# The last chunk's normalisation on ScalarE and VectorE in place of GpSimd, stored by halves on two queues

## The chip, the cores and the metric

The kernel runs on one core of one Trainium2 chip. The metric is the device time of one execution in microseconds (us), taken outside the profiler; several executions are made and their median is quoted. A separate, profiled execution gives the rows that are read below. The engines are called by the profile's names: PE is TensorE (PEld its weight loads), DVE is VectorE, ACT is ScalarE, POOL is GpSimd, SP is SyncE, which here only issues transfers and waits. A "q" behind a name (POOLq, SPq) marks instructions that the engine's sequencer handles: waits, barriers, drains, issues of transfers.

## The reference

A transformer layer of two parts, each followed by a residual sum and a normalisation over the 512 columns of a row without learned parameters. The input x has 4 batches of 1024 rows of 512 columns, all in fp32.

```
def _layernorm(x, axis=-1, eps=1e-05):
    m = jnp.mean(x, axis=axis, keepdims=True)
    v = jnp.var(x, axis=axis, keepdims=True)
    return (x - m) / jnp.sqrt(v + eps)
...
    x = _layernorm(x + _L0_attn_ref(x, L0_attn_wq, L0_attn_wk, L0_attn_wv, L0_attn_wo), axis=-1)
    x = _layernorm(x + _L0_ffn_ref(x, L0_ffn_A, L0_ffn_B, L0_ffn_Wr, L0_ffn_br), axis=-1)
```

`_L0_attn_ref` is softmax attention with 16 heads of 32 columns. `_L0_ffn_ref` picks for each row the one of 8 experts with the largest router logit; an expert is a product down to 64 columns (A) and back up to 512 (B), weighted with the router's probability. What matters here is only the very last step of the second line: the second normalisation of the last rows.

## The kernel before

The kernel walks over units of (batch, group of four heads). A planner at the end of the function lays out steps; to each step it assigns matrix products of the attention and pieces of the projections and of the expert stage of earlier batches, so that TensorE always has work. The instructions of one engine run in the order in which the code emits them (`keep_order` ties them down).

For the first three batches the expert stage (`class After`) sorts rows by expert; its results go out with indirect stores issued by GpSimd (L649). For the last batch (`class Last`) the rows stay where they are. Its 1024 rows are handled in four chunks of 256 rows (`n` = 0 to 3, `NQ` = 4), each of two tiles of 128 rows (`i` = 0, 1). `down(i, half)` multiplies the masked inner values with the second expert matrix for one half of the columns (256, four matmuls, L743), and VectorE adds gate times result to the rows `h` (L747). In the first three chunks the norm follows for whole tiles. In the last chunk (`self.n == NQ - 1`, the code from L755 on) nothing is left to hide anything under, so the statistics are taken by halves: `bn_stats` on each half as it comes (L757), `bn_aggr` over both (L760) once the second half is there, giving mean and variance.

From there the norm before the change runs over three engines. VectorE negates the mean (L761). `finish_stats` on GpSimd adds eps (L407), raises to the power -0.5 (L408) and multiplies with the negated mean (L409). `apply` on ScalarE computes scale times h plus bias over all 512 columns (L419). `store` sends the 128x512 tile out on SyncE's queue (L766). Tile 0 of the last chunk goes through this while TensorE still multiplies for tile 1; tile 1 goes through it alone.

GpSimd's last work ahead of these two tiles are four indirect stores of the third batch (L649). After the last instruction of the kernel's body every engine runs a closing sequence that the framework adds, recorded under L1113: SyncE waits for every counter that a transfer or an engine still owes, one wait after the other; each engine drains; all meet at a barrier that GpSimd opens, which is followed by a reset of the semaphores and a second barrier.

On-chip memory is handed out by pools in the order of first use: `const` (one buffer each) and then `work` (two buffers unless stated). Sizes are rounded up to 32 bytes per partition.

Of the kernel before, what the change touches and what calls it, by code (L numbers as in the profile page):

```python
# [9 lines left out]
F32 = mybir.dt.float32  # L10
# [3 lines left out]
AF = mybir.ActivationFunctionType  # L14
ALU = mybir.AluOpType
# [3 lines left out]
P = 128  # L19
# [4 lines left out]
EPS = 1e-5  # L24
# [17 lines left out]
def attention_then_experts(  # L42
# [18 lines left out]
    pe, act, dve, pool, sync = nc.tensor, nc.scalar, nc.vector, nc.gpsimd, nc.sync  # L61
    B, S, D = x.shape
# [4 lines left out]
    TQ = QC // P  # L67
# [4 lines left out]
    H2 = D // 2  # L72
# [8 lines left out]
    const = ctx.enter_context(tc.tile_pool(name="const", bufs=1))  # L81
    work = ctx.enter_context(tc.tile_pool(name="work", bufs=2))
# [7 lines left out]
    def bank():  # L90
        turn_of[0] += 1
        return banks[(turn_of[0] - 1) % len(banks)]
# [31 lines left out]
    pool.memset(ones, 1.0)  # L124
    power = const.tile([P, TQ], F32, tag="power", name="power")
    pool.memset(power, -0.5)

    rev = const.tile([P, TQ, E], F32, tag="rev", name="rev")
    for e in range(E):
# [5 lines left out]
        out=before_f,  # L135
# [33 lines left out]
    for t in spread_m:  # L169
# [5 lines left out]
        out=expand_f,  # L175
# [226 lines left out]
    def finish_stats(mv):  # L402

        n = mv.shape[1]
        rs = work.tile([P, 2, TQ], F32, tag="rs", name="rs", bufs=4)[:, :, :n]
        var = work.tile([P, TQ], F32, tag="var", name="var")[:, :n]
        pool.tensor_scalar_add(var, mv[:, :, 1], EPS)  # L407
        pool.tensor_tensor(rs[:, 0], var, power[:, :n], ALU.pow)  # L408
        pool.tensor_tensor(rs[:, 1], mv[:, :, 0], rs[:, 0], ALU.mult)  # L409
        return rs  # L410
# [7 lines left out]
    def apply(h, rs, i):  # L418
        act.activation(h, h, AF.Identity, bias=rs[:, 1, i : i + 1], scale=rs[:, 0, i : i + 1])  # L419
# [42 lines left out]
    def stored(i):  # L462

        for other in stores:
            tc.declare_no_dep(i, other, reason="other rows")
        stores.append(i)

    class After:
# [159 lines left out]
        def down(self, k):  # L628
            tiles = [bank() for _ in range(2)]
            for i, ps in enumerate(tiles):  # L630
                pe.matmul(ps, self.u[k][ts(i, R), :], self.wb[k][ts(i, R), :], start=True, stop=True)  # L631
            for i, ps in enumerate(tiles):
                t = self.x[k, i]
                dve.scalar_tensor_tensor(t[:, :D], ps, t[:, D : D + 1], t[:, :D], ALU.mult, ALU.add)
# [35 lines left out]
    class Last:  # L670
# [69 lines left out]
        def down(self, i, half):  # L740
            ps = bank()[:, :H2]
            for k in range(C):
                pe.matmul(  # L743
                    ps, self.u[:, k, ts(i, P)], places["wd"][:, k, ts(half, H2)], start=(k == 0), stop=(k == C - 1)
                )
            h = self.h[i][:, ts(half, H2)]
            dve.scalar_tensor_tensor(h, ps, self.gate[:, i : i + 1], h, ALU.mult, ALU.add)  # L747
            if self.n < NQ - 1:
                if half == 1:
                    if i == 0:  # L750
                        self.mv = work.tile([P, TQ, 2], F32, tag="y_mv", name="y_mv2")
                    self.add(self.mv, i)
                return

            if half == 0:  # L755
                self.st = work.tile([P, 2, 6], F32, tag="st2", name="st2")
            dve.bn_stats(self.st[:, half, :], h)  # L757
            if half == 1:
                mv = work.tile([P, 1, 2], F32, tag="y_mv3", name="y_mv3")
                dve.bn_aggr(mv[:, 0, :], self.st)  # L760
                dve.tensor_scalar_mul(mv[:, 0, 0:1], mv[:, 0, 0:1], -1.0)  # L761
                apply(self.h[i], finish_stats(mv), 0)
                self.store(i)

        def store(self, i):
            stored(sync.dma_start(out[B - 1, ts(TQ * self.n + i, P), :], self.h[i]).ins)  # L766
# [116 lines left out]
    for b, r in enumerate(rest):  # L883
        end = start_of(C * b + C)
        for i in range(4):
            part = sorted_x[b].rearrange("(i j p) w -> i p j w", p=P, i=4)[i]
# [4 lines left out]
        for t in range(NT):  # L891
            n, i = divmod(t, TQ)
# [224 lines left out]
```

## Time and profile before

| what | value |
| --- | --- |
| median of 3 runs | 1482.48 us (1482.31 to 1485.71) |
| the profiled execution: time | 1484.24 us |
| the profiled execution: span from first to last instruction | 1482.5 us |
| granted TensorE clock, mean | 0.998 |
| start of VectorE's last sum (L747), behind the last matmul | 1473.07 us |
| end of ScalarE's last norm (L419) | 1476.36 us |
| issue of the last store (L766) | 1476.38 us |
| transfers in the last 43 us: SyncE's queue | 1.05 MB, 5.6% of 16 engines |

Times with two decimals are positions in the span of the profiled execution, in us from its first instruction. A row of the timeline gives start and length, then engine, line, operation, what is written and read, and in brackets how long the engine had been idle before it and who ended that. A row of an instruction group gives the shortest, median and longest length in ns and the first and last start. The time before is that of whole executions; the span is shorter than the profiled execution's time by what lies around it (1484.24 - 1482.5 = 1.7 us).

### The profile page before, as it was taken

How to read it: one execution, taken by the hardware profiler on the slowest of the kernel's cores; microseconds unless marked ns; L12 is line 12 of the kernel's file. 1: busy time of each engine (PE TensorE's matmuls, PEld its weight loads, DVE VectorE, ACT ScalarE, POOL GpSimd, SP SyncE). 2: the span in 40 equal slices, each digit the busy share in tenths (PEclk: the TensorE clock that was granted, in tenths of full speed). 3: DMA queues.
4: the chain of work that ended last, by engine and by line, in shares of the span. 5: the costliest groups of instructions: out<-in, count | busy, mean ns of one | idle time of the engine just before them, and what ended most of it. 6: DMA issues, size and time to landing. Idle time of an engine off the chain costs nothing.

```text
span 1482.5 us, 36966 instructions
## 1 busy us (share of the span) xinstructions
PE 1448.4 (98%) x15091; PEld 947.9 (64%) x15091; DVE 984.3 (66%) x1822; ACT 743.1 (50%) x1519; POOL 1170.3 (79%) x918
## 2 busy tenths in 40 slices
PE   8999999999999999999999999999999999999997
PEld 6666666666666666666666666666666655666665
DVE  1556666665767567776776656777676767777764
ACT  1125555554444555555444455555544555456552
POOL 2019999998977989999987888999997899999302
PEclk9999999999999999999999999999999999999999
DMA  7422121114001622433200333342411230222010
GB/s 242 137 82 81 47 70 60 56 44 155 18 30 41 193 90 86 130 100 123 73 16 29 101 122 101 119 130 88 158 30 30 73 115 23 69 74 70 20 37 29
DMA packets 93050, 122.09 MB, mean 82 GB/s; under 512 B 7607, under 2 KB 68039, under 8 KB 92880
## 3 DMA queue, kind: packets, MB, share of 16 engines
q1 hardware_dynamic: 84672, 103.93, 22.3%
q0 software_dynamic: 6096, 13.69, 2.5%
q8 instruction: 119, 1.95, 0.6%
q10 hardware_dynamic: 2112, 2.10, 0.4%
q14 instruction: 51, 0.42, 0.1%
HBM read 92.34 MB, written 33.63 MB: 85 GB/s over the span
## 4 chain that ended last, share of the span: by engine, by line
PE 84%; POOL 7%; ACT 4%; issue 2%; DMA 1%; DVE 1%; ACTq 0%; POOLq 0%; SPq 0%
PE bank L373 14%; PE bank L330 13%; PE bank L290 12%; PE bank L276 8%; PE bank L257 8%; PE bank L267 8%; PE bank L454 7%; POOL dens L358 5%; PE bank L321 5%; ACT probs L340 3%; PE bank L392 2%; PE bank L729 2%; PE bank L622 1%; PE bank L615 1%; PE bank L631 1%
## 5 line engine op out<-in xcount | busy, mean ns | idle before, releaser
L358 POOL TENSOR_TENSOR dens<-dens,probs 128x1024 f32<-128x1024 f32 x360 | 849.0, 2358 | 79.3 <-ACT probs L340 57.1
L292 DVE TENSOR_REDUCE top<-bank 128x1 f32<-128x512 f32 x1024 | 635.9, 683 | 407.5 <-PE bank L290 407.2
L340 ACT ACTIVATE probs<-bank 128x512 f32<-128x512 f32 x1024 | 528.1, 603 | 284.6 <-PE bank L330 264.7
L290 PE MATMUL bank<-k,q 32*128 32x512 f32 x2048 | 276.9, 593 | 0.0
L330 PE MATMUL bank<-q,k 32*128 32x256 f32 x4096 | 266.2, 374 | 0.0
L373 PE MATMUL bank<-probs,v 128*32 128x256 f32 x4096 | 234.3, 380 | 0.0
L330 PEld LDWEIGHTS bank<-q,k 32*128 32x128 f32 x4096 | 201.0, 184 | 18.2 <-issue 2.3
L373 PEld LDWEIGHTS bank<-probs,v 128*32 128x32 f32 x4096 | 131.7, 110 | 91.4 <-ACT probs L340 14.1
L350 POOL TENSOR_TENSOR dens<-probs 128x1024 f32<-128x1024 f32 x60 | 141.3, 2355 | 5.6 <-ACT probs L340 5.3
L257 PE MATMUL bank<-xT,wq 128*128 128x256 f32 x512 | 128.6, 395 | 9.9 <-DMA xT<-in_xt 6.4
L257 PEld LDWEIGHTS bank<-xT,wq 128*128 128x128 f32 x512 | 93.5, 192 | 58.8 <-ACT probs L340 37.4
L276 PE MATMUL bank<-wv,xT 128*128 128x256 f32 (+1 forms) x512 | 125.6, 392 | 1.7 <-ACT probs L340 1.1
L267 PE MATMUL bank<-xT,wk 128*128 128x256 f32 x512 | 125.1, 389 | 1.0 <-ACT probs L340 0.9
L454 PE MATMUL bank<-wo,aT 128*128 128x264 f32 (+1 forms) x512 | 122.2, 389 | 3.0 <-ACT probs L340 2.9
L395 DVE RECIPROCAL bank<-bank 128x256 f32<-128x256 f32 x64 | 112.6, 1759 | 12.9 <-PE bank L392 12.9
L290 PEld LDWEIGHTS bank<-k,q 32*128 32x128 f32 x2048 | 107.7, 184 | 18.6 <-issue 5.6
L267 PEld LDWEIGHTS bank<-xT,wk 128*128 128x128 f32 x512 | 95.5, 192 | 37.1 <-ACT probs L340 25.1
L276 PEld LDWEIGHTS bank<-wv,xT 128*128 128x128 f32 x512 | 93.6, 190 | 38.9 <-ACT probs L340 20.6
L454 PEld LDWEIGHTS bank<-wo,aT 128*128 128x128 f32 x512 | 94.6, 190 | 36.3 <-ACT probs L340 20.3
L381 ACT COPY both<-bank 128x256 f32<-128x256 f32 x64 | 23.8, 372 | 179.2 <-PE bank L373 175.2
L321 PE MATMUL bank<-mT,ones_b 3*128 3x512 bf16 x1024 | 106.1, 384 | 1.9 <-ACT probs L340 0.9
L321 PEld LDWEIGHTS <-ones_b 3*128 3x128 bf16 x1024 | 27.0, 91 | 89.9 <-issue 89.6
(129 smaller groups left out, 993.8 us busy)
## 6 DMA issues: line engine op xcount, KB each, us to landing
xT<-in_xt SPq DMA_DIRECT2D x98, 512.0 KB, 3.6
sorted<-nothing SPq DMA_DIRECT2D x12, 1028.0 KB, 6.9
x<-sorted SPq DMA_DIRECT2D x48, 257.0 KB, 3.5
h<-in_x SPq DMA_DIRECT2D x32, 256.0 KB, 3.9
wa<-in_wa SPq DMA_DIRECT2D x48, 128.0 KB, 2.3
wb<-in_wb SPq DMA_DIRECT2D x48, 128.0 KB, 3.2
out<-h SPq DMA_DIRECT2D x8, 256.0 KB, 2.0
wo<-in_wo POOLq DMA_DIRECT2D x1, 1024.0 KB, 6.2
```

Source lines behind the costliest of these rows:

```text
L257: pe.matmul(ps, wq_sb[:, c, ts(units[u][1], P)], x.x[:, c, :], start=(c == 0), stop=(c == C - 1))
L267: pe.matmul(ps, wk_sb[:, c, ts(units[u][1], P)], x.x[:, c, :], start=(c == 0), stop=(c == C - 1))
L276: pe.matmul(ps, x.x[:, c, ts(t, P)], wv_sb[:, c, columns(h)], start=(c == 0), stop=(c == C - 1))
L290: pe.matmul(ps, q[r, ts(t % TQ, P)], kT[u][r, ts(n, 512)], start=True, stop=True)
L292: dve.tensor_reduce(top[i][:, here // 2, j, n : n + 1], ps, axis=AX.X, op=ALU.max, negate=True)
L321: pe.matmul(ps.rearrange("p (k q) -> p k q", q=QC), ones_b[r, :], m[r, :].unsqueeze(1).to_broadcast((NP, 2, QC)), start=True, stop=False,)
L330: pe.matmul(ps[:, ts(k, QC)], kT[u][r, ts(2 * kp + k, P)], qT[u, c][r, :], start=False, stop=(k == 1),)
L340: act.activation(pr[:, :, j, :], ps.rearrange("p (k q) -> p k q", q=QC), AF.Exp)
L350: adder.tensor_add(dens[u, c], pr[:, 0].rearrange("p j q -> p (j q)"), pr[:, 1].rearrange("p j q -> p (j q)"),)
L358: adder.tensor_add(dens[u, c], dens[u, c], pr[:, k].rearrange("p j q -> p (j q)"))
L373: pe.matmul(ps[j * HD : (j + 1) * HD, :], v[:, k, col : col + HD], probs[u, c, k // 2][:, k % 2, j, :], start=(k == 0), stop=(k == NK - 1),)
L454: pe.matmul(ps, aT[b, c, n][:, ts(i, P)], wo_sb[:, c, columns(half)], start=(c == 0), stop=(c == C - 1))
```

## The change

A constant `eps` of 128x1 is added among the constants. In the last chunk the negation and the calls of `finish_stats`, `apply` and `store` go. Instead ScalarE takes the square root of variance plus eps (128x1), VectorE the reciprocal, and VectorE computes (h - mean) times that, in two instructions of 256 columns each. Each half is stored as soon as it is ready: the first on SyncE's queue, the second on ScalarE's. `finish_stats`, `apply` and `store` stay for all other rows.

```
     power = const.tile([P, TQ], F32, tag="power", name="power")
     pool.memset(power, -0.5)
+    eps = const.tile([P, 1], F32, tag="eps", name="eps")
+    pool.memset(eps, EPS)
...
             dve.bn_stats(self.st[:, half, :], h)
             if half == 1:
-                mv = work.tile([P, 1, 2], F32, tag="y_mv3", name="y_mv3")
-                dve.bn_aggr(mv[:, 0, :], self.st)
-                dve.tensor_scalar_mul(mv[:, 0, 0:1], mv[:, 0, 0:1], -1.0)
-                apply(self.h[i], finish_stats(mv), 0)
-                self.store(i)
+                mv = work.tile([P, 2], F32, tag="y_mv3", name="y_mv3")
+                dve.bn_aggr(mv, self.st)
+                rs = work.tile([P, 1], F32, tag="rs3", name="rs3")
+                act.activation(rs, mv[:, 1:2], AF.Sqrt, bias=eps)
+                dve.reciprocal(rs, rs)
+                row = ts(TQ * self.n + i, P)
+                for part, queue in enumerate((sync, act)):
+                    h = self.h[i][:, ts(part, H2)]
+                    dve.tensor_scalar(h, h, mv[:, 0:1], rs, ALU.subtract, ALU.mult)
+                    stored(queue.dma_start(out[B - 1, row, ts(part, H2)], h).ins)
```

`stored` declares that stores write different rows, so that they don't wait for each other. The square root needs another table of ScalarE's functions than the exponential, so the built program holds a second ACT_TABLE_LOAD, in front of the first square root. All lines behind the constants move down by two.

## The prediction

> **What bounds the kernel now.** I read the page's busy shares and its chain of waits first, then the timeline of the last 9 us, then the instructions of L1113, which is where the program's closing barrier is recorded.
>
> ```profile
> PE 1448.4 (98%) x15091; PEld 947.9 (64%) x15091; DVE 984.3 (66%) x1822; ACT 743.1 (50%) x1519; POOL 1170.3 (79%) x918
> ...
> PE 84%; POOL 7%; ACT 4%; issue 2%; DMA 1%; DVE 1%; ACTq 0%; POOLq 0%; SPq 0%
> ```
>
> TensorE is busy for 98% of the span. The change touches nothing in front of the last chunk's norm, so it can only act on what follows the last matmuls, and there the timeline (start, length) is a chain through four engines:
>
> ```profile
> 1473.07 0.48 DVE L747 SCALAR_TENSOR_TENSOR h<-bank,gate,h 128x256 f32<-128x256 f32 x1 [0.78 <-PE bank L743]
> 1473.59 0.43 DVE L757 BATCH_NORM_STATS2 st<-h 128x6 f32<-128x256 f32 x1
> 1474.06 0.21 DVE L760 BATCH_NORM_AGGREGATE y_mv<-st 128x2 f32<-128x12 f32 x1
> 1474.30 0.15 DVE L761 TENSOR_SCALAR y_mv<-y_mv 128x1 f32<-128x1 f32 x1
> 1474.35 0.23 POOL L407 TENSOR_SCALAR var<-y_mv 128x1 f32<-128x1 f32 x1 [2.30 <-DVE y_mv L760]
> 1474.66 0.58 POOL L408 TENSOR_TENSOR rs<-var,power 128x1 f32<-128x1 f32 x1
> 1475.32 0.19 POOL L409 TENSOR_TENSOR rs<-y_mv,rs 128x1 f32<-128x1 f32 x1
> 1475.55 0.81 ACT L419 ACTIVATE h<-h,rs 128x512 f32<-128x512 f32 x1 [2.64 <-POOL rs L409]
> 1476.38 0.33 SPq L766 DMA_DIRECT2D out<-h  x1
> ```
>
> The store lands 2.0 us after its issue, at 1478.4. The span ends at 1482.5, 4.1 us later, and the chain of waits stops at L419 and does not say why. The instructions of L1113 between 1475 and 1481, and between 1481 and 1481.85, do:
>
> ```profile
> L1113 SPq EVENT_SEMAPHORE  x9: 28/28/28, 1476.8 to 1478.4; - x9
> L1113 SPq DRAIN  x2: 7/7/7, 1478.5 to 1478.5; - x2
> L1113 POOLq DRAIN  x1: 6445/6445/6445, 1475.3 to 1475.3; - x1
> ...
> L1113 POOLq EVENT_SEMAPHORE  x1: 17/17/17, 1481.8 to 1481.8; - x1
> ```
>
> SyncE has seen every transfer land and has arrived at the barrier at 1478.5. GpSimd's closing DRAIN starts at 1475.3, behind L408, and lasts 6.445 us, to 1481.7; only then (1481.8) does GpSimd open the barrier, and 0.8 us later all is over. So what **ends last is GpSimd's drain, not the last store**: the store has 3.3 us to spare. In the rows GpSimd's last arithmetic (L409) ends at 1475.51, 6.2 us before the drain does.
>
> **The change part by part.** Instruction order on all five engines is the same up to the last chunk's norm, but for one more memset (eps, 128x1) among those before the first matmul; the rows of that kind take 0.10 us and TensorE waits for a DMA until 5.97 us, so that costs nothing.
>
> *Removed from GpSimd:* L407 to L409 for both tiles, its only work behind the indirect stores of L649, whose last one starts at 1466.4 and takes 0.98 us. Its closing drain can then start at about 1467.4. If its length is a price paid once behind the last GpSimd instruction, it ends at 1467.4 + 6.4 = 1473.8, or 1475.2 if it waits first for the slowest landing of these stores (2.1 to 3.6 us by their row). Both lie under the chain above; to come back onto the path it would have to grow past 10 us. No row shows what the drain waits for; its bounds are the rivals below.
>
> *The new path,* from the end of L760 (1474.27), for the second tile:
> - to ScalarE 0.08 (the hop from L760 to GpSimd's L407: 1474.27 to 1474.35).
> - Sqrt on 128x1. Not in the trace: at least 0.16 (L435, 16 columns from a PSUM bank), at most 0.35 (L419's 0.81 less 512 columns at 0.90 ns, the slope between L730 at 357 ns and L707 at 588). It reads SBUF and a pointer operand as L419 does, with one pointer less: 0.30.
> - back to VectorE 0.04 (L409 to L419: 1475.51 to 1475.55), reciprocal 0.17 (L446, 166 ns), gap 0.04 (L757 to L760).
> - norm of 128x256 on VectorE: between 0.15 (L761, the same operation on one column) and 0.48 (L747, 256 columns with a PSUM operand). Nearest is L757, which reads the same half tile from SBUF: 0.43. The second half doesn't wait for the first; the two L448 take 0.21 for 0.15 each, so it ends 0.35 later.
>
> Sum: 0.08 + 0.30 + 0.04 + 0.17 + 0.04 + 0.43 + 0.35 = 1.41; the second half is ready at 1475.68, where L419 now ends at 1476.36. L761 goes too, but lies beside L407 today.
>
> A rule that would make this shorter: the Trainium skill, "VectorE: DVE Perf Modes", section "The perf-mode tier table (the rule you actually need)", gives tensor_scalar on fp32 in SBUF two results a cycle (1227 ns for 2048 columns). No row of this trace has such an operation on more than one column. By that rule a half would be some 0.13 us shorter, an estimate from that page, and the forecast would be 1478.4 instead of 1478.8.
>
> *The wait it adds on VectorE.* The first tile's reciprocal now sits in VectorE's queue and waits for ScalarE; behind it stand the two halves and then the second tile's L747. First tile: L760 ends at 1470.81, plus 1.41 is 1472.22; L747, L757 and gaps (0.04 + 0.48 + 0.04 + 0.43 + 0.04) bring 1473.25, where the last L747 starts at 1473.07 today. Late by 0.18, or by nothing with the low price of the norm: I take 0.12. Behind ScalarE's first store, which waits for that norm (1472.2), stands only the second Sqrt, needed at 1474.35: free.
>
> *Table load.* One ACT_TABLE_LOAD (1283 ns in the row of L259) now precedes the first Sqrt. In the built order it follows the last L730, which ends at 1465.9, and carries no wait; ScalarE then sits idle until 1472.09 ("6.14 <-POOL rs L409"), so it is over near 1467.2, 3.6 us before it is needed. Nothing, unless it waits with its Sqrt (a rival).
>
> *Stores.* Four of 128 KB for two of 256 KB; the second half goes out on ScalarE's queue, whose issue at the kernel's start took no longer than SyncE's. Ready to issue 0.05. Today's landing is 2.03. In the window of the last 43 us four 256 KB stores and nothing else take 5.6% of 16 engines, 0.60 us a store; half of it saves 0.30: 1.73, with 2.3 (the longest landing of the four stores) as the other end. The last landing: 1475.68 + 0.12 + 0.05 + 1.73 = 1477.58.
>
> *The closing waits.* SyncE waits for the landings one by one. Its last of nine waits is today for the last store; in the changed program ScalarE's last store is the fourth of ten, so six waits follow the landing at 0.063 us (eight from 1476.77 to 1477.21): 0.38. Today that would lie under the drain, now it is on the path. Then drain and arrival 0.12 (1478.41 to 1478.53), the message to GpSimd 0.06, the barrier 0.8: 1477.58 + 0.38 + 0.12 + 0.06 + 0.8 = **1478.9**, against 1482.5: **3.6 us less**. The profiled execution took 1484.24 us with its span of 1482.5; what lies around the span isn't touched. On the median of 1482.48 that makes **1478.8**. Low prices (0.14 Sqrt, 0.28 for a norm half, no lateness 0.12) give 1478.2; high ones (landing +0.57, Sqrt +0.05, lateness +0.06, ScalarE's first issue in 1400 us +0.1) 1479.6.
>
> **The rivals.**
> - *The drain doesn't move (B).* It may be tied to something else: to the last landing (1478.4 to 1481.7 is 3.3 us: the new end is 1477.6 + 3.3 + 0.8 = 1481.7), or to the last indirect stores, which stay where they are (end unchanged, 1482.5). Then the change doesn't do what it says, since GpSimd still ends last. For: the opening drain on GpSimd (L1106) took 0.168 us, so the long one pays for something that came in between. Against: GpSimd issues none of the last stores, and between the indirect ones and the drain L407 to L409 run at their usual lengths. 1481.6 to 1482.5.
> - *The table load waits with its Sqrt (D).* The Trainium skill, "ScalarE: Activation LUTs", section "Table sets: the hidden batching unit", speaks against an exp kernel that calls sqrt once: the load is placed right before the activation. As a mechanism: the first tile's Sqrt ends 1.28 us later, VectorE's queue carries all of it to the second tile, 1478.8 + 1.28 = 1480.1. Against: the built order, and 4.9 us of idle.
> - *Slower (C): the 32 bytes.* eps takes a 32-byte slot, and every tile allocated behind it, all working tiles with probs, dens, q, k, v among them, moves by 32 bytes, off multiples of 64. If that cost TensorE 1 ns a matmul, 15091 of them are 15.1 us: 1478.8 + 15.1 = 1493.9. It eats the gain from 0.24 ns (3.6 / 15091) on. For: half the wo rows that L454 reads already start 32 bytes past a multiple of 64 (rows of 2080 bytes), and it takes 388 ns to L729's 386. Against: L257, with all its rows on multiples of 64, takes 395.
>
> **How the numbers follow.** A measurement of this kernel can't tell less than some 0.3% (4.45 us: the bounds are 1478.03 and 1486.93) from no change. The forecast (A, the drain goes under cover) has 0.71: the row of the drain is the only thing behind 1478.5. Its own range is 1477.8 to 1479.7; the low prices and the scatter between runs put 0.24 of it under 1478.03. B has 0.16, D 0.04, C 0.09. Faster: 0.24. Same: 0.47 of A, B and D, together 0.67. Slower: C, 0.09. A's own range leaves out too much (B, C, part of A), so the range reaches over D and B: 1477.6 to 1482.5.
>
> **What would show it.** In the changed profile GpSimd's long DRAIN starts near 1467.4 and ends before 1476; GpSimd's barrier instruction follows SyncE's arrival by less than 0.1 us; SyncE shows six waits behind the last landing; the last L747 starts 0 to 0.2 us later than today after its matmul; ACT_TABLE_LOAD stands near 1466. The prediction is wrong if the drain still ends last, or if matmul lengths in the body differ.

## The result, and the profile after

| | before | after |
| --- | --- | --- |
| median of 8 runs each (three of those of before were known ahead of the prediction) | 1484.86 us (1482.31 to 1486.66) | 1480.47 us (1479.12 to 1482.42) |
| ratio of the times | | 0.9975, 95% interval 0.9966 to 0.9984 |
| the profiled execution: time, span | 1484.24, 1482.5 us | 1481.49, 1479.8 us |
| start of VectorE's last sum (L747; L749 after) | 1473.07 us | 1474.16 us |
| from there to the end of the span | 9.47 us | 5.62 us |

The ratio makes 3.7 us less (0.0025 x 1484.86; 2.4 to 5.0 by the interval). In the profiled pair the stretch behind the last sum is 3.85 us shorter, and the body ahead of it 1.09 us longer. The body is taken up behind the experiments; the change acts on the stretch.

The busy shares and the chain of waits of the kernel after (its page):

```profile
PE 1449.9 (98%) x15091; PEld 950.9 (64%) x15091; DVE 985.5 (67%) x1826; ACT 743.1 (50%) x1520; POOL 1168.2 (79%) x913
...
PE 73%; POOL 17%; issue 4%; ACT 3%; DMA 1%; DVE 1%; ACTq 0%; POOLq 0%; SPq 0%; DVEq 0%
```

The busy shares hardly differ from those of before, as they must: 3.85 us are 0.26% of the span, and a share in whole per cents cannot show that. The shares of the chain do differ (PE 73% for 84%, POOL 17% for 7%), but these are shares of the whole span, whose body the change does not touch; why the chain runs back another way there was not followed up, and nothing below rests on it. The five instructions fewer on GpSimd (913 for 918) are L407 to L409 of two tiles less the memset of eps. What changed is seen in the timeline of the end (start, length):

```profile
1474.16 0.48 DVE L749 SCALAR_TENSOR_TENSOR h<-bank,gate,h 128x256 f32<-128x256 f32 x1
1474.68 0.43 DVE L759 BATCH_NORM_STATS2 st<-h 128x6 f32<-128x256 f32 x1
1475.14 0.21 DVE L762 BATCH_NORM_AGGREGATE y_mv<-st 128x2 f32<-128x12 f32 x1
1475.38 0.29 ACT L764 ACTIVATE rs<-y_mv,eps 128x1 f32<-128x1 f32 x1 [3.16 <-DVE y_mv L762]
1475.71 0.16 DVE L765 RECIPROCAL rs<-rs 128x1 f32<-128x1 f32 x1 [0.36 <-ACT rs L764]
1475.91 0.74 DVE L769 TENSOR_SCALAR h<-h,y_mv,rs 128x256 f32<-128x256 f32 x2
1476.35 0.33 SPq L770 DMA_DIRECT2D out<-h  x1
1476.74 0.36 ACTq L770 DMA_DIRECT2D out<-h  x1
```

From the end of the statistics (1475.35) to the end of the norm (1476.65) it is 1.30 us; before it was 2.09 (1474.27 to 1476.36). That alone would have been worth nothing, since the old store had 3.2 us to spare (SyncE's arrival at 1478.53 to GpSimd's opening of the barrier at 1481.77). The rest is in the closing sequence, recorded under L1120 now. First GpSimd's last instruction, then the closing sequence's instructions between 1466 and 1479, then those of all the run for GpSimd's semaphores:

```profile
1467.44 0.97 POOL L651 DMA_INDIRECT out<-x  x1 [0.30 <-issue]
...
L1120 SPq EVENT_SEMAPHORE  x10: 28/28/28, 1476.7 to 1478.9; - x10
L1120 SPq DRAIN  x2: 7/7/7, 1478.9 to 1479.0; - x2
L1120 POOLq DRAIN  x1: 8063/8063/8063, 1466.6 to 1466.6; - x1
...
L1120 POOLq EVENT_SEMAPHORE  x4: 17/17/17, 1479.0 to 1479.7; - x4
```

GpSimd's drain begins at 1466.55 instead of 1475.3. It is 8.06 us long instead of 6.45, yet ends at 1474.6, because the last indirect store still runs at its start and ends at 1468.41: from there the drain takes 6.20 us, as it took 6.2 from the end of L409 before. SyncE arrives at 1478.98 and GpSimd opens the barrier 0.03 us later, where SyncE used to wait 3.24 us for it. The drain is now done 4.4 us before anyone needs it. Of the 3.85 us, 3.21 are this wait. The other 0.64 are the shorter way from the last sum to SyncE's arrival (4.82 us for 5.46): the shorter norm and store, which count only because the wait is gone.

### The profile page after: what moved, and what is told of

It reads as the page before. It is cut to its first block, busy times and chain, and to the rows that moved or that the text cites. A ratio compares the mean times of both kernels' runs of the same rounds, so it can differ in the third digit from the quotient of the medians.

```text
span 1479.8 us, 36968 instructions
## 1 busy us (share of the span) xinstructions
PE 1449.9 (98%) x15091; PEld 950.9 (64%) x15091; DVE 985.5 (67%) x1826; ACT 743.1 (50%) x1520; POOL 1168.2 (79%) x913
## 3 DMA queue, kind: packets, MB, share of 16 engines
q0 software_dynamic: 6096, 13.69, 2.5%
## 4 chain that ended last, share of the span: by engine, by line
PE 73%; POOL 17%; issue 4%; ACT 3%; DMA 1%; DVE 1%; ACTq 0%; POOLq 0%; SPq 0%; DVEq 0%
POOL dens L360 13%; PE bank L375 11%; PE bank L332 11%; PE bank L292 10%; PE bank L278 7%; PE bank L456 7%; PE bank L269 7%; PE bank L259 7%; PE bank L323 4%; ACT probs L342 3%; PE bank L394 2%; POOL dens L352 1%; PE bank L731 1%; DMA xT<-in_xt 1%; PE bank L745 1%
```

## The experiments

Two theories compete for the main gain. By the first, GpSimd's drain is a price that begins behind GpSimd's last instruction, wherever that stands, so that taking the two tiles' root off GpSimd moved it; open within it is what sets the length, a fixed price or so much for each transfer that GpSimd issued. By the second, the drain is beside the point and the shorter norm or the two queues made the gain. Then come the terms of the norm and the store, and last the 32 bytes. "Stretch" is the time from the start of VectorE's last sum to the end of the span; it leaves out how long the body took. Edits are against the kernel after, unless said otherwise.

**One small GpSimd instruction put back** (e1_pool_touch), one for each of the last chunk's two tiles, used by nobody:

```
                 dve.reciprocal(rs, rs)
+                spare = work.tile([P, 1], F32, tag="spare", name="spare")
+                pool.tensor_scalar_add(spare, mv[:, 1:2], EPS)
```

> The changed kernel with one more GpSimd instruction in each of the last two tiles (variance plus eps, 128x1, into a tile that nobody reads), waiting for the same bn_aggr as ScalarE's root. Theory 1, the closing drain takes some 6.2 us behind GpSimd's last instruction, whatever that is: the drain ends 6.2 us behind the new instruction, GpSimd opens the barrier last again, and the stretch from the start of VectorE's last sum to the end of the span grows from 5.6 us (changed kernel) to about 8.5 us, that is +2.9 us; nearly all of the gain is gone though nothing waits for the added instruction. Theory 2, the drain's end is tied to the last indirect stores or to the last landing: the stretch stays at 5.6 us.

The stretch is 8.52 us: 2.90 of the 3.85 us are gone, though the norm and the stores are the new ones. The time is 1485.01 us, 0.9997 of before (0.9987 to 1.0007), no longer clear of it. The last GpSimd instruction of this kernel's timeline, and GpSimd's part of the closing sequence between 1470 and 1484:

```profile
1476.29 0.22 POOL L767 TENSOR_SCALAR spare<-y_mv 128x1 f32<-128x1 f32 x1 [3.22 <-DVE y_mv L762]
...
L1122 POOLq EVENT_SEMAPHORE  x4: 17/17/17, 1482.8 to 1483.4; - x4
L1122 POOLq DRAIN  x3: 51/103/6480, 1476.2 to 1483.3; - x3
```

A 0.22 us instruction that nothing waits for moves the drain to 1476.24 to 1482.72, 6.22 us behind its own end. The barrier opens right behind that, at 1482.8. So GpSimd's last instruction sets the end, whether it belongs to the norm or not. The 0.95 us that are left of the gain follow from the same: it ends 1.49 us behind the start of the last sum, where L409 ended 2.44 behind it. The shorter norm and the two queues are in this kernel too, and change nothing while GpSimd finishes late; the norm without GpSimd is the means, GpSimd's early finish the gain.

**What sets the drain's length.** Three kernels differ in how many transfers GpSimd issues: 75 in the kernels before and after (24 scatters of sorted rows, 48 indirect stores, 3 direct loads).

No indirect transfers (e2_no_indirect), 3 are left:

```
-            i = pool.indirect_dma_start(
-                out=sorted_x[self.b],
...
+            self.h.pop(t)
...
-                i = pool.indirect_dma_start(
-                    out=out_rows,
...
+                pass
```

> The changed kernel without its 24 indirect scatters and 48 indirect stores (the results of the first three batches are left out); GpSimd still issues 3 direct transfers at the start. Theory 1a, the drain's 6.2 us are a fixed price: its end lies 6.2 us behind GpSimd's last instruction. Theory 1b, the price grows with the number of transfers that GpSimd has issued in the run (75 for 6.2 us, 0.083 us each): 3 transfers give 0.25 us. Theory 1c, it is paid only where an indirect transfer ran: near 0.05 us, as the drain at the start of the kernel.

A quarter of the indirect stores (e3_few_indirect), 39 transfers:

```
                 t = self.x[k, i]
+                if k >= 2:
+                    continue
                 i = pool.indirect_dma_start(
                     out=out_rows,
```

> The changed kernel with 12 of its 48 indirect stores (the results of three quarters of the rows of the first three batches are left out), so GpSimd issues 39 transfers for 75. Theory 1a (fixed): the drain ends 6.2 us behind GpSimd's last instruction. Theory 1b (per transfer, 0.083 us each): 3.2 us behind it. Theory 1c (paid at all or not): 6.2 us.

Every scatter twice (e4_more_indirect), the second time into a spare buffer, 99 transfers:

```
...
+            d = pool.indirect_dma_start(
+                out=extra_x[self.b],
+                out_offset=bass.IndirectOffsetOnAxis(ap=self.slot[:, t : t + 1], axis=0),
+                in_=self.h.pop(t),
...
```

> The changed kernel with every indirect scatter issued a second time, to a second buffer that nobody reads: 99 transfers from GpSimd for 75. Theory 1a (fixed) and 1c: the drain ends 6.2 us behind GpSimd's last instruction. Theory 1b (per transfer): 8.2 us behind it.

The last GpSimd instruction of each and its drain (the longest where a row has two), from the timeline and from the closing sequence, in this order:

```profile
1459.85 0.20 POOL L411 TENSOR_TENSOR rs<-y_mv,rs 128x2 f32<-128x2 f32 x1
...
L1099 POOLq DRAIN  x2: 107/342/578, 1459.8 to 1475.1; - x2
```

```profile
1465.67 0.19 POOL L411 TENSOR_TENSOR rs<-y_mv,rs 128x2 f32<-128x2 f32 x1
...
L1122 POOLq DRAIN  x1: 3512/3512/3512, 1465.6 to 1465.6; - x1
```

```profile
1495.52 0.97 POOL L664 DMA_INDIRECT out<-x  x1 [0.30 <-issue]
...
L1133 POOLq DRAIN  x1: 10025/10025/10025, 1494.6 to 1494.6; - x1
```

The recorded lengths count from where the sequencer took the drain up, while the last instruction was still running. From the end of that instruction (start plus length in the rows) to the end of the drain:

| transfers that GpSimd issued | drain behind GpSimd's last instruction | 0.10 + 0.0816 x transfers |
| --- | --- | --- |
| 3 | 0.34 us | 0.34 |
| 39 | 3.28 us | 3.28 |
| 75 (after; e1_pool_touch) | 6.20; 6.22 us | 6.22 |
| 99 | 8.17 us | 8.18 |

Two numbers fit five kernels within 0.02 us. So the price grows with what GpSimd issued in the whole run; the fixed price falls. It isn't a wait for landings: in e1_pool_touch the last indirect store starts at 1468.29 and lands 3.6 us later, long before the drain begins at 1476.24. In e2_no_indirect and e3_few_indirect, too, the last instruction ahead of the drain is arithmetic, in the two others it is an indirect store, and all lie on one line.

What is counted stays open. The queue whose packets go with these transfers (q0 on the pages of e2_no_indirect, e3_few_indirect, after and e4_more_indirect: packets, MB, share of the 16 engines) moved:

```profile
q0 software_dynamic: 336, 1.07, 0.3%
q0 software_dynamic: 3216, 9.63, 1.8%
q0 software_dynamic: 6096, 13.69, 2.5%
q0 software_dynamic: 8016, 20.01, 3.7%
```

One number, 1.02 ns a packet, fits as well: 0.34, 3.28, 6.22 and 8.18 us. Every indirect transfer here has 80 packets, so these runs cannot tell a price per packet from one per transfer; bytes do not fit (1.07, 9.63, 13.69 and 20.01 MB).

Times of one execution each: 1477.52 us without indirect transfers, 1483.26 with 39, 1509.57 with 99. These move with the work left out or added in the body and say nothing of the drain, which is under cover in all three (the execution with 24 more scatters is some 27 us longer).

**The norm over a whole tile** (e5_whole_tile), one instruction of 512 columns and one store of 256 KB on SyncE's queue:

```
-                row = ts(TQ * self.n + i, P)
-                for part, queue in enumerate((sync, act)):
-                    h = self.h[i][:, ts(part, H2)]
-                    dve.tensor_scalar(h, h, mv[:, 0:1], rs, ALU.subtract, ALU.mult)
-                    stored(queue.dma_start(out[B - 1, row, ts(part, H2)], h).ins)
+                h = self.h[i]
+                dve.tensor_scalar(h, h, mv[:, 0:1], rs, ALU.subtract, ALU.mult)
+                self.store(i)
```

> The changed kernel with the norm in one VectorE instruction of 512 columns and one store of 256 KB on SyncE's queue for each tile, instead of two of each. Theory 1, by the changed kernel's rows: the norm costs 0.41 + 0.27 = 0.68 us for 0.74 us of both halves (0.06 less), the landing 2.03 for 1.76 us (0.27 more), and the counter of the last store is again the last that SyncE waits for, so the 0.36 us of six waits behind the landing go: the stretch from VectorE's last sum to the end shrinks from 5.63 to about 5.4 us. The halves then bring nothing. Theory 2, the halves and the second queue are worth the second half's norm and half a landing, 0.3 us or more: the stretch grows to 5.9 us or more.

The stretch is 5.29 us, 0.34 less than with halves. The norm and the issue in its timeline:

```profile
1476.35 0.55 DVE L767 TENSOR_SCALAR h<-h,y_mv,rs 128x512 f32<-128x512 f32 x1
1476.92 0.33 SPq L771 DMA_DIRECT2D out<-h  x1
```

The norm took less than the 0.68 us expected, hence 5.29 for 5.4: 512 columns take 0.546 us, 256 take 0.414: 0.52 ns a column and 0.28 us that each instruction pays whatever its width. The norm of the tile is ready 0.55 us after its start instead of 0.74. SyncE sees the store land 2.035 us after its issue, 0.27 later than the half's 1.76, but its counter is the last that SyncE asks for, so the six waits behind the landing (0.363) are gone. The gap to the issue is 0.03 for 0.087. So 0.19, 0.36 and 0.06 are gained and 0.27 lost: 0.34, as seen. One execution: 1481.58 us beside 1482.52 for the kernel before.

**The six waits moved ahead of the landing** (e6_last_counter). Transfers take their counters in turn; the first load of wq is cut into seven pieces, which turns the order so that the last store's counter is asked for last:

```
-    load_wq(sync, slice(P, D))
+    cuts = [P, 192, 256, 320, 368, 416, 464, D]
+    for a, b in zip(cuts, cuts[1:]):
+        load_wq(sync, slice(a, b))
```

> The changed kernel with one load of the first weights at the kernel's start split into seven, which turns the round of transfer counters so that ScalarE's last store owns the one that SyncE waits for last. Theory 1, the six waits behind the last landing are paid in full: the stretch from VectorE's last sum to the end shrinks from 5.63 to about 5.27 us, and no wait lies between the last landing and SyncE's drain. Theory 2, SyncE's waits overlap something else that ends then: 5.6 us.

The stretch is 5.27 us, 0.35 less, and no wait stands behind the last landing. It also shows what e5_whole_tile won: with the counter asked for last, two halves on two queues (5.27) are as fast as the whole tile (5.29). There, the 0.19 of the norm and the 0.06 of the gap go for the 0.27 of the longer landing, and the place of the counter is the gain. One execution: 1482.66 us beside 1482.52; the body was 1.5 us longer than that of after, which stays unexplained.

**Both halves on SyncE's queue** (e7_one_queue):

```
-                for part, queue in enumerate((sync, act)):
+                for part, queue in enumerate((sync, sync)):
```

> The changed kernel with both halves stored on SyncE's queue. SyncE's issue of the first half of the last tile (0.33 us) ends some 0.04 us after the second half is normed. Theory 1, the second queue is worth next to nothing: the stretch from VectorE's last sum to the end stays within 0.1 us of 5.63 us. Theory 2, two transfers on one queue follow each other: the second landing comes 0.3 us or more later, and the stretch is 5.9 us or more.

The stretch is 5.675 us for 5.624, 0.05 more. The two issues of the last tile in the timeline:

```profile
1475.25 0.81 SPq L770 DMA_DIRECT2D out<-h  x2
```

They follow one another within 0.81 us, and since the second half becomes ready 0.32 us behind the first, the second issue hardly has to wait. The second queue is worth 0.05 us. One execution: 1480.43 us.

**Root and reciprocal in one** (e8_rsqrt):

```
-                act.activation(rs, mv[:, 1:2], AF.Sqrt, bias=eps)
-                dve.reciprocal(rs, rs)
+                act.activation(rs, mv[:, 1:2], AF.Abs_reciprocal_sqrt, bias=eps)
```

> The changed kernel with ScalarE's Abs_reciprocal_sqrt in place of Sqrt, and without VectorE's reciprocal. Theory 1: the reciprocal's 0.164 us and one gap of 0.036 us lie on the path, so the stretch from VectorE's last sum to the end shrinks by 0.2 us, from 5.63 to 5.43 us; the table load stays hidden. Theory 2, ScalarE's instruction or its table takes longer by as much: 5.6 us.

The stretch is 5.42 us: the reciprocal (0.164) and its gap are gone, and the function costs what Sqrt cost (0.294). One execution: 1479.45 us.

**Both halves issued at once** (e11_split_store): root and reciprocal in one, one norm of 512 columns, then the two halves on the two queues, with the first load cut as above:

```
-                act.activation(rs, mv[:, 1:2], AF.Sqrt, bias=eps)
-                dve.reciprocal(rs, rs)
+                act.activation(rs, mv[:, 1:2], AF.Abs_reciprocal_sqrt, bias=eps)
+                dve.tensor_scalar(self.h[i], self.h[i], mv[:, 0:1], rs, ALU.subtract, ALU.mult)
...
                     h = self.h[i][:, ts(part, H2)]
-                    dve.tensor_scalar(h, h, mv[:, 0:1], rs, ALU.subtract, ALU.mult)
```

> As the run with the reciprocal root, but with the norm of 512 columns in one VectorE instruction and its store split into two halves that go out on SyncE's and ScalarE's queues at the same time; the first weights' load is split into seven as in the run on the counters, so that no long row of waits follows the landing. Theory 1, both queues feed the same 16 engines, so two halves at once land as late as one store of 256 KB (2.0 us): the stretch is about 5.1 us. Theory 2, two queues move at twice the rate, and each half lands in 1.76 us: about 4.9 us.

The stretch is 5.21 us, 0.1 above the figure of the first theory and longer than with one store (5.08, next). Both halves are issued at 1474.54, and SyncE sees the later one land at 1476.645: some 2.1 us, against 2.03 for the 256 KB in one store and 1.76 for a half alone. So the second theory falls: two queues at once move the tile no faster than one. Of the 0.14 us more than with one store, 0.08 are the landing and 0.06 one more wait of SyncE behind it. One execution: 1479.33 us.

**The best of these together** (e9_whole_rsqrt): the whole tile of e5_whole_tile with the function of e8_rsqrt.

```
-                act.activation(rs, mv[:, 1:2], AF.Sqrt, bias=eps)
-                dve.reciprocal(rs, rs)
...
+                act.activation(rs, mv[:, 1:2], AF.Abs_reciprocal_sqrt, bias=eps)
+                h = self.h[i]
+                dve.tensor_scalar(h, h, mv[:, 0:1], rs, ALU.subtract, ALU.mult)
+                self.store(i)
```

> Two findings together: Abs_reciprocal_sqrt on ScalarE without VectorE's reciprocal, and norm and store of a whole tile at once (one VectorE instruction of 512 columns, one store on SyncE's queue). Theory 1, the two gains add up: the stretch from VectorE's last sum to the end is 5.62 - 0.34 - 0.20 = 5.08 us, 4.4 us less than before the change, a ratio of about 0.997 to the kernel before, 0.5 us better than the changed kernel. Theory 2, the drain or another wait takes over: 5.3 us or more.

The stretch is 5.08 us, 0.54 less than after. The three steps behind the statistics are left:

```profile
1472.76 0.29 ACT L764 ACTIVATE rs<-y_mv,eps 128x1 f32<-128x1 f32 x1 [3.16 <-DVE y_mv L762]
1473.09 0.55 DVE L766 TENSOR_SCALAR h<-h,y_mv,rs 128x512 f32<-128x512 f32 x1 [0.36 <-ACT rs L764]
1473.66 0.33 SPq L770 DMA_DIRECT2D out<-h  x1
```

The time is 1481.2 us, 0.9980 of before (0.9971 to 0.9989), where about 0.997 was expected. Half a microsecond is 0.04% of the time, less than the half-width of that interval (0.09%): the trace shows it, the times can't.

**The 32 bytes** (e10_eps_only): the kernel before with the constant and nothing else, so that only the working tiles move:

```
     pool.memset(power, -0.5)
+    eps = const.tile([P, 1], F32, tag="eps", name="eps")
+    pool.memset(eps, EPS)
```

> The kernel before with the constant eps alone added (128x1, read by nobody), which moves all later tiles by 32 bytes. Theory 1, the address has no price: the time is that of the kernel before within 0.2%, the matmul rows keep their means, the stretch from VectorE's last sum to the end stays 9.47 us. Theory 2 (rival C of the prediction), 1 ns a matmul: some 15 us slower.

The stretch is 9.47 us, that of before. The time is 1485.57 us, 1.0012 of before (1.0003 to 1.0021): between 0.4 and 3 us slower, nowhere near the 15 us of 1 ns a matmul. The means of the three largest matmul groups, two thirds of all matmuls, are those of before (593, 374 and 380 ns); the next two have 398 for 395 and 387 for 389. The difference goes with the clock: the mean granted clock of these ten executions is 0.9956, that of the 21 beside them 0.9968. A loss of 0.0012 of 1485 us is some 1.7 us, an estimate, and the medians lie 1.6 us apart.

The other way round (e12_no_shift): e9_whole_rsqrt with eps in a spare column of an older tile, so that all tiles stand where they stood before:

```
-    power = const.tile([P, TQ], F32, tag="power", name="power")
-    pool.memset(power, -0.5)
-    eps = const.tile([P, 1], F32, tag="eps", name="eps")
+    power = const.tile([P, TQ + 1], F32, tag="power", name="power")
+    pool.memset(power[:, :TQ], -0.5)
+    eps = power[:, TQ:]
```

> The version with the reciprocal root and whole tiles, but with eps in a third column of the tile power, whose slot of 32 bytes has room for it, so that all tiles stand where they stood in the kernel before. Theory 1, the moved addresses cost nothing: the ratio to the kernel before is 0.998 to 0.997 as with them moved (0.9980, interval 0.9971 to 0.9989), the stretch from VectorE's last sum to the end 5.08 us. Theory 2, the moved addresses cost the body some 1 to 2 us (eps alone gave 1.0012): the ratio falls to 0.9970 or less, the stretch is the same.

1481.61 us, 0.9976 of before (0.9967 to 0.9985), stretch 5.08. Its interval and that of e9_whole_rsqrt overlap for the most part, and the 0.9970 of the second theory lies inside it: this pair does not decide.

**What the body does on its own.** Two windows of 20 us of the kernel before, then of the kernel after (busy time of each engine, granted TensorE clock, DMA share, GB/s):

```profile
1200.00:1220.00 20.00, 17.96 (x232) 10.82 (x228) 12.62 (x20) 11.73 (x24) 18.98 (x14) 1.00 0.52 160
1400.00:1420.00 20.00, 19.06 (x218) 12.43 (x220) 13.12 (x23) 13.59 (x28) 4.25 (x7) 1.00 0.19 67
```

```profile
1200.00:1220.00 20.00, 17.54 (x209) 10.82 (x204) 12.04 (x18) 10.62 (x22) 19.24 (x14) 0.91 0.51 159
1400.00:1420.00 20.00, 19.07 (x202) 12.40 (x201) 11.73 (x21) 13.21 (x27) 3.86 (x7) 0.91 0.21 67
```

In each of the two windows the clock of the kernel after is 0.91, and fewer matmuls are done (202 for 218 in the second). Two shorter windows of the kernel after show how the loss is shared out in the first:

```profile
1204.00:1208.00 4.00, 1.54 (x20) 0.70 (x16) 2.48 (x4) 2.21 (x5) 3.71 (x7) 0.88 0.76 214
1208.00:1212.00 4.00, 4.00 (x48) 2.34 (x44) 0.88 (x2) 2.26 (x5) 3.84 (x3) 0.69 0.75 241
```

The clock is at half for 3.41 us. Where TensorE is busy throughout, such a stretch should cost half its length: 1.7 us, an estimate (0.12 x 4 + 0.31 x 4 = 1.72 by these rows). The profiled executions of kernels with this body (so without e2_no_indirect, e3_few_indirect and e4_more_indirect) have none, one or two of them ahead of the last sum, mostly near the same two times:

| kernel | tiles moved | start of the last sum | half-clock stretches ahead of it | less 1.71 us for each |
| --- | --- | --- | --- | --- |
| before | no | 1473.07 | none | 1473.07 |
| e12_no_shift | no | 1473.96 | at 1412 | 1472.25 |
| after | yes | 1474.16 | at 1207, 1412 | 1470.75 |
| e1_pool_touch | yes | 1475.01 | at 1413 | 1473.31 |
| e5_whole_tile | yes | 1474.60 | at 1412 | 1472.89 |
| e6_last_counter | yes | 1475.69 | at 1209, 1414 | 1472.28 |
| e7_one_queue | yes | 1473.06 | at 1207 | 1471.35 |
| e8_rsqrt | yes | 1472.33 | none | 1472.33 |
| e9_whole_rsqrt | yes | 1471.54 | none | 1471.54 |
| e10_eps_only | yes | 1476.35 | at 21, 1414 | 1472.94 |
| e11_split_store | yes | 1472.42 | none | 1472.42 |

With them taken off, the nine moved kernels lie between 1470.75 and 1473.31 (mean 1472.2), the two others at 1472.25 and 1473.07. The profiles show no price of the 32 bytes, and the 0.4 to 3 us of the timed pair of e10_eps_only go with its lower clock. Whether the move costs up to about 1 us of 1480, or itself lowers the clock, stays open. So does why the clock halves in one execution and not in the next: near 1205 TensorE is idle for 2.0 to 2.5 us in all eleven, with a half-clock stretch behind it in three, and near 1412 it is idle for 0.45 us in all, with one in six.

## Why the prediction held, step by step

- *The mechanism.* Right: GpSimd's drain ended last, starts behind GpSimd's last work, and went under cover; e1_pool_touch puts it back and takes 2.90 of the 3.85 us away. It ends at 1474.6 where 1473.8 was written: the indirect stores end 1 us later in this execution (1468.41 for 1467.4), as the body does, and from there the drain took 6.20 us for the 6.4 of the sum. "A price paid once behind the last GpSimd instruction" is right as to once and as to where; what it is paid for was open: 0.0816 us for each transfer that GpSimd issued, or as well 1.02 ns for each of their packets.
- *The sum.* Forecast 3.6 us less, seen 3.85 in the profiled pair and 3.7 (2.4 to 5.0) in the times. The figure of 1478.8 stood on a median of 1482.48 from three runs; over eight runs the kernel before has 1484.86, so the 1480.47 of after lies 1.7 above the figure though the difference is as forecast. It lies outside the forecast's own range (1477.8 to 1479.7), inside the wide one only, and nearer to rival D's 1480.1 than to 1478.8: the time alone could not have told which mechanism ran, the rows of the profile do. That the stretch came out within 0.25 us of the sum is no luck of one term: the lateness and the arithmetic were 0.12 and 0.11 too dear, and the other terms, each off by 0.04 or less to either side, by 0.01 together.
- *Lateness of the last sum,* 0.12: the one term that wasn't there. L749 starts 0.039 us behind its matmul as L747 did. The sum had VectorE's queue arrive 0.18 late at full prices. Two things took that away: the first tile's path was 0.11 shorter, and VectorE's sum for the first half of tile 1 starts 0.09 before the recorded end of the norm (1473.11; 1472.46 + 0.74 = 1473.20 in the rows below), where a gap of 0.04 was added. So VectorE is through with that half at 1474.05 (its statistics start at 1473.62 and take 0.43), 0.07 before the last matmul ends at 1474.12.
- *Hops and arithmetic,* 1.41: 1.30. Hop to ScalarE 0.034 (0.08: hops from VectorE to GpSimd are no measure for it), Sqrt 0.294 (0.30), back 0.033 (0.04), reciprocal 0.164 (0.17), gap 0.036 (0.04), half 0.415 (0.43), second half 0.32 (0.35).
- *Store and closing waits.* Ready to issue 0.087 (0.05), landing 1.76 (1.73), six waits 0.363 (0.38), to the arrival 0.122 (0.12), message 0.033 (0.06), barrier 0.77 (0.8). The landing of a half was the widest bound, 2.3, and came out where halving the transfer's share put it.
- *The Trainium skill's rule for the norm.* The trace shows 0.52 ns a column on 128x512 against 128x256. The Trainium skill, "VectorE: DVE Perf Modes", section "The perf-mode tier table (the rule you actually need)", gives two results a cycle for this operation, 1227 ns for 2048 columns, which is 0.60 ns a column with all fixed parts in it; the slope agrees with that. A half still took 0.415 us and not 0.13 less, since 0.28 us of it does not depend on the width: the forecast from the nearest row held for a half, and the rate would have held for the difference between a half and a whole tile. Two halves pay the fixed part twice, which is why the norm of a whole tile is 0.19 us shorter than that of two halves.
- *Rival B* (the drain doesn't move) falls with the drain's end at 1474.6, 3.9 us ahead of the last landing. What spoke for it, that the long drain pays for something which came in between, was true: it pays for transfers, but at the place where GpSimd stops.
- *Rival D* (the table load waits with its Sqrt) falls. ScalarE's rows and VectorE's between 1466.9 and 1475:

```profile
1467.05 1.28 ACT L764 ACT_TABLE_LOAD   x1
...
1471.93 0.29 ACT L764 ACTIVATE rs<-y_mv,eps 128x1 f32<-128x1 f32 x1 [3.60 <-DVE y_mv L762]
...
1472.46 0.74 DVE L769 TENSOR_SCALAR h<-h,y_mv,rs 128x256 f32<-128x256 f32 x2
...
1473.11 0.48 DVE L749 SCALAR_TENSOR_TENSOR h<-bank,gate,h 128x256 f32<-128x256 f32 x1
```

The load starts behind ScalarE's last copy and is over at 1468.33; ScalarE is idle for 3.60 us until the Sqrt. In the order the load stands ahead of its Sqrt, as the Trainium skill says ("ScalarE: Activation LUTs", section "Table sets: the hidden batching unit": a load is put before every activation that needs one). In time the two lie 3.60 us apart.

- *Rival C* (1 ns a matmul from the 32 bytes, 15 us) falls with e10_eps_only. A price of some 1 us in all is neither shown nor ruled out.
- *The signs named.* GpSimd's barrier instruction follows SyncE's arrival by 0.033 us, six waits stand behind the last landing, the last sum is not late, and the table load stands at 1467.05. The one sign against, other matmul lengths in the body, shows no price of the 32 bytes: the five largest groups keep their means within 1 ns, and L731 has 400 ns for 386 in this execution with its half-clock stretch near 1412, where single ones take up to 797.

## What to carry to other kernels

Look at what the closing sequence waits for before shortening the last store: here the store had 3.2 us to spare, and an engine's drain ended last. Where GpSimd has issued transfers, let its last instruction of any kind come early enough for the drain, 0.10 us and 0.0816 for each transfer, to end ahead of the last landing; in this kernel some 54 more transfers of 80 packets (4.4 / 0.0816) would fill the cover that is left, an estimate that keeps GpSimd's last instruction where it is. Behind that, see which counter is asked for last: with the last store's counter last, one wide instruction and one store (5.29 us) and two halves on two queues (5.27) came out alike, and the whole tile has less code.

## What the hardware showed that was not expected

- GpSimd's drain grows with the transfers that it issued in the run, landed long ago or not: 0.34 us for 3, 8.17 us for 99 (or with their packets: 336 and 8016).
- Two queues that store half a tile each, issued in the same moment, land in 2.1 us; one queue takes 2.03 for the whole tile.
- SyncE's closing waits take 0.06 us each even when their transfers have landed, so the place of the last store's counter among them is worth up to 0.36 us.
- The clock goes to half for 3.41 us near the same times (1207 and 1412) in some executions and not in others; that is 1.7 us each time, an estimate. Without them the eleven starts of the last sum spread over 2.6 us instead of 4.8.
